# Two stacked graph attentions: graph 0's unmasked attention by product for half of its targets and by prefix tables for the rest, with graph 1's first steps moved ahead of period 0

## The chip, the cores and the metric

The kernel runs on one core of a Trainium2 chip. The metric is the device time of one execution in microseconds (us); the lower the better. All data are float32.

## What is computed

For each of 16 graphs with 1024 nodes of 256 features (one adjacency matrix for all), two layers, each added to its input:

```python
# layer 0 (slope 0.2)
h   = relu(layernorm(x))
out = relu(h @ mlp1_w + mlp1_b)                  # 256 -> 512
res = out
out = gat(relu(out), None, W_fc, a_fc)           # every node attends to every node
out = elu(out) + res
out = relu(out @ mlp2_w + mlp2_b)                # 512 -> 256
res = out
out = gat(relu(out), adj, W_hand, a_hand)        # masked by adj
x   = x + relu(elu(out) + res)
# layer 1 (slope 0.01)
h   = relu(layernorm(x))
x   = x + relu(masked attention of h @ W)

def gat(inp, mask, W, a):
    h = inp @ W
    e = leaky_relu(f1[:, None] + f2[None, :])    # f1 = h @ a[:F], f2 = h @ a[F:]
    return elu(softmax(where(mask, e, -big)) @ h)
```

## The kernel before, in words

A fast path does the whole work; a general path behind a flag is for inputs of a very wide range and does not run here. All line numbers are those of the profile.

**Unmasked attention, two ways.** The weight of source j for target i depends only on f1[i] + f2[j], and leaky_relu has two branches. So if the nodes are sorted by f2, each target's numerator is one prefix sum over the sorted rows of one branch plus one suffix sum of the other. Graphs 1 to 15 do this (class `Dense`): VectorE counts each node's rank (`rank`, L472 to L487), GpSimd scatters the rows of h to their places in memory by indirect DMA (`scatter`, L492), the sync queue reads them back sorted (`read_sorted`, L528), VectorE makes running sums over the eight rows of each partition (`sum_before`, `sum_behind`, L547 to L567), which are written to memory as the fine table (`write_before`, `write_behind`, L557, L570); TensorE adds up the totals of the partitions (`carry`, L578), written as the coarse table. ScalarE finds each target's place by summing signs (`sign`, L516; `count`, L521), GpSimd gathers one fine and one coarse row for each target (`gather`, L589; the coarse gather adds into the fine one's rows), and `share` and `mean` (L599 to L609) divide. Graph 0 doesn't: `vectors`, `query_row`, `weight`, `product`, `product_mean` (L612 to L657) make the 1024 x 1024 weights and multiply them with h on TensorE, eight target tiles of 128 (tile `od`).

**Around it.** `Norm` does the layer norm (statistics `stats`, root `root` on GpSimd, `center`, `turn`: transposes, L250 to L275). `mlp1` (L428), `project` (h for the attention, L442), `merge` and `merge_end` (transposes hpT, elu and the residual add on GpSimd, L664 to L675), `mlp2` (L682). `Masked`, with `Gnn0` and `Gnn1`, is the masked attention of layers 0 and 1: `project` (L309), weights (L354), `product` (tiles oa and ob, L365), `finish`, `combine` (Gnn0's two adds on GpSimd, L387 and L388), `update` (L392, L405).

**Order of the work.** Every step is put into a list with a time of its own by `at(lo, hi, steps)`; the list is sorted by these times and traced in this order, and each engine runs its instructions in the order of the trace. The times are no durations: they only settle the order on each engine. GpSimd's instructions are tied to one another in this order too (L932 to L944), only scatters may stand loosely among themselves. The graphs are staggered: in period b (142 units) TensorE does the first masked product of graph b, the second masked product of graph b - 1, the merges and mlp2 of graph b + 1, and mlp1 and `project` of graph b + 2. Before period 0 stands a prologue (L863 to L899): mlp1 and projection of graph 0, the masks, graph 0's product, its merges and mlp2, mlp1 of graph 1 and its projection, with graph 1's ranks and scatters (`dense_begin`) from 28 units before period 0. Graph 1's sums (`dense_sums`) and gathers (`dense_end`) stand in period 0. Period 0 has no second masked product.

**Buffers.** Tags with few buffers make later tiles wait for earlier ones: "seq" (two: sorted rows, sums, gathered rows, h), "att" (eight weight tiles), "hn" (four), PSUM "mm" (four) and "tr" (two).

The lines that fix the prologue and the stagger:

```python
    base = -1 * PERIOD
    at(base - 6, base + 8, each(d.project, range(NT), [1]))
    at(base + 8, base + 22, each(d.project, range(NT), [0]))
    for t in range(NT):
        lo = base + 40 + 7.1 * t
        at(lo, lo + 7, each(d.product, [t], range(NT)))
    merges(base + 71, d, 0)
    merges(base + 99.2, d, 1)
    second_mlp(base, 0)
    dense_begin(base + PERIOD, 1)
```

Of the kernel before, what the change touches and what calls it, by code (L numbers as in the profile page):

```python
# [8 lines left out]
F32 = mybir.dt.float32  # L9
# [22 lines left out]
def fast_path(ctx: ExitStack, tc: tile.TileContext, alarm, x, adj, w1, b1, w2, b2, w_fc, a_fc,  # L32
# [49 lines left out]
    def load_x(b, name):  # L82
        xt = big.tile([P, NT, F], F32, tag="x", name=f"{name}_{b}", bufs=3)
        nc.sync.dma_start(xt, x[b].rearrange("(t p) f -> p t f", p=P))
        return xt
# [284 lines left out]
    class Gnn0(Masked):  # L370
        ONES = 2

# [10 lines left out]
        def combine(self, t, o_nat):  # L383
            e, pos = self.out[t]
            nc.scalar.activation(e, e, AF.Exp, scale=-1.0)
            nc.scalar.activation(e, e, AF.Exp, bias=neg1)  # L386
            nc.gpsimd.tensor_add(pos, pos, o_nat[:, t, :])  # L387
            nc.gpsimd.tensor_add(e, e, pos)  # L388
            self.out[t] = e
# [21 lines left out]
    class Dense:  # L411


        def __init__(self, b):
# [6 lines left out]
            self.dens = {}  # L421

# [96 lines left out]
        def count(self):  # L519
            self.k = k = small.tile([P, 2, NT], I32, tag="k", name=f"k_{self.b}")  # L520
            nc.vector.tensor_scalar(k[:, 0, :], self.signs, -0.5, N / 2, op0=OP.mult, op1=OP.add)  # L521
            nc.vector.tensor_scalar(k[:, 1, :], k[:, 0, :], 3, None, op0=OP.arith_shift_right)

        def read_sorted(self):
            self.xs = big.tile([P, NT, R], F32, tag="seq", name=f"xs_{self.b}", bufs=2)
            rows = sorted_d[self.b % 2].rearrange("(p r) f -> p r f", p=P)
            for h in range(2):
                reader = nc.sync.dma_start(self.xs[:, half(h)], rows[:, half(h)])  # L528
# [4 lines left out]
        def sums_begin(self):  # L533
            b = self.b
            self.bd = small.tile([P, 2, NT], F32, tag="bd", name=f"bd_{b}")
            self.tt = big.tile([P, NT, K], F32, tag="seq", name=f"tt_{b}", bufs=2)
            self.all_t = work.tile([P, K], F32, tag="part", name=f"all_{b}")
            nc.gpsimd.memset(self.tt[:, 0, :], 0.0)

        def sums_weights(self, h):  # L540
            f2 = self.xs[:, half(h), K]
# [5 lines left out]
        def sum_before(self, r):  # L547
            xs, bd, tt = self.xs, self.bd, self.tt
            if r == 0:
                nc.vector.tensor_scalar(tt[:, 1, :], xs[:, 0, :K], bd[:, 1, 0:1], None, op0=OP.mult)  # L550
            else:
                nc.vector.scalar_tensor_tensor(tt[:, r + 1, :] if r + 1 < NT else self.all_t,
                                               xs[:, r, :K], bd[:, 1, r:r + 1], tt[:, r, :],
                                               op0=OP.mult, op1=OP.add)

        def write_before(self):
            nc.sync.dma_start(fine_d[self.b % 2][:N, :K].rearrange("(p r) f -> p r f", p=P),  # L557
                              self.tt)

        def sum_behind(self, r):  # L560
            xs, bd = self.xs, self.bd
            if r == NT - 1:
                nc.vector.tensor_scalar(xs[:, r, :K], xs[:, r, :K], bd[:, 0, r:r + 1], None,
                                        op0=OP.mult)
            else:
                nc.vector.scalar_tensor_tensor(xs[:, r, :K], xs[:, r, :K], bd[:, 0, r:r + 1],  # L566
                                               xs[:, r + 1, :K], op0=OP.mult, op1=OP.add)  # L567

        def write_behind(self):
            nc.sync.dma_start(fine_d[self.b % 2][:N, K:].rearrange("(p r) f -> p r f", p=P),  # L570
                              self.xs[:, :, :K])

        def carry(self, s):
            lhsT, total = ((upto, self.all_t), (after, self.xs[:, 0, :]))[s]
# [9 lines left out]
        def gather(self, h, coarse, u):  # L584
            if h not in self.got:
                self.got[h] = big.tile([P, TH, 2 * K], F32, tag="seq", name=f"got_{self.b}_{h}",
                                       bufs=2)
            t = h * TH + u
            nc.gpsimd.indirect_dma_start(  # L589
                out=self.got[h][:, u, :], out_offset=None,  # L590
# [4 lines left out]
        def share(self, h):  # L595
            got = self.got[h]
            qh = self.q[:, h * TH:(h + 1) * TH]
            den = self.dens[h] = small.tile([P, 2, TH], F32, tag="den", name=f"den_{self.b}_{h}")
            nc.vector.tensor_mul(den[:, 0, :], got[:, :, F], qh)  # L599
            nc.vector.tensor_add(den[:, 0, :], den[:, 0, :], got[:, :, K + F])  # L600
            nc.vector.reciprocal(den[:, 0, :], den[:, 0, :])
            nc.vector.tensor_mul(den[:, 1, :], den[:, 0, :], qh)

        def mean(self, h, u):
            got, den, name = self.got[h], self.dens[h], f"{self.b}_{h}_{u}"
            part = work.tile([P, K], F32, tag="part", name=f"part_{name}")
            nc.scalar.activation(part, got[:, u, :K], AF.Copy, scale=den[:, 1, u:u + 1])
            hp = self.hps[h, u] = work.tile([P, K], F32, tag="hp", name=f"hp_{name}", bufs=TH)
            nc.vector.scalar_tensor_tensor(hp, got[:, u, K:], den[:, 0, u:u + 1], part,  # L609
                                           op0=OP.mult, op1=OP.add)  # L610

        def vectors(self):  # L612

            b, f1, f2 = self.b, self.fs[:, 0, :], self.fs[:, 1, :]
            ext_ps = tr_psum(f"extdps_{b}")
            row_broadcast(ext_ps[:, :P], [self.ext])
            top = small.tile([P, 3], F32, tag="topd", name=f"topd_{b}")
            nc.vector.tensor_reduce(top[:, 0:1], ext_ps[:, :P], AX.X, OP.max)
            nc.vector.tensor_scalar(top[:, 1:2], top[:, 0:1], -1.0, None, op0=OP.mult)
            nc.vector.tensor_scalar(top[:, 2:3], top[:, 0:1], -SLOPE_A, None, op0=OP.mult)  # L620
            self.q = small.tile([P, NT], F32, tag="qd", name=f"qd_{b}")
            nc.vector.tensor_scalar(self.q, f1, top[:, 0:1], 0.0, op0=OP.add, op1=OP.max)
            nc.scalar.activation(self.q, self.q, AF.Exp, scale=SLOPE_A - 1.0)
# [762 lines left out]
```

## Time and profile before

| | us |
|---|---|
| median of 3 runs | 2419.56 (2419.07 to 2420.93) |
| the profiled execution | 2418.14 |
| its span in the trace | 2416.4 |
| TensorE busy | 2331.7 |
| VectorE busy | 1611.9 |
| ScalarE busy | 1280.2 |
| GpSimd busy | 965.5 |

The profile is one execution. In the 40 slices of the span a digit is the busy share of a slice in tenths, and PEclk is the granted TensorE clock in tenths. In rows of a timeline stand start, duration, engine, line, operation, out<-in, the number of instructions (x), and in brackets the idle time before and what ended it. A float32 matmul of the program shows as two records. A name such as oa or hpT leaves out the buffer numbers: oa is graph b's first masked product, ob its second, od graph 0's unmasked one, nt a norm's transposes, m an mlp's sum. Times that follow each other on an engine overlap by some tenths of a microsecond.

### The profile page before, as it was taken

How to read it: one execution, taken by the hardware profiler on the slowest of the kernel's cores; microseconds unless marked ns; L12 is line 12 of the kernel's file. 1: busy time of each engine (PE TensorE's matmuls, PEld its weight loads, DVE VectorE, ACT ScalarE, POOL GpSimd, SP SyncE). 2: the span in 40 equal slices, each digit the busy share in tenths (PEclk: the TensorE clock that was granted, in tenths of full speed). 3: DMA queues.
4: the chain of work that ended last, by engine and by line, in shares of the span. 5: the costliest groups of instructions: out<-in, count | busy, mean ns of one | idle time of the engine just before them, and what ended most of it. 6: DMA issues, size and time to landing. Idle time of an engine off the chain costs nothing. (4 is left out here: it accounts for less than half of the span.)

```text
span 2416.4 us, 31367 instructions
## 1 busy us (share of the span) xinstructions
PE 2331.7 (96%) x10393; PEld 1809.2 (75%) x10393; DVE 1611.9 (67%) x4455; ACT 1280.2 (53%) x2723; POOL 965.5 (40%) x1214
## 2 busy tenths in 40 slices
PE   7999699999999999999999999999999999999897
PEld 5777478787887878788787778878777787878666
DVE  6247377685866768586676858667685866758554
ACT  4236454565655456564545656454565645455442
POOL 1013436344353634435363443536344353634320
PEclk9999799999999999999999999999999999999898
DMA  5005637255472725547272554727265472726500
GB/s 183 1 1 156 167 108 193 75 175 132 149 192 106 192 78 172 134 147 194 100 193 79 172 139 138 203 96 195 77 172 143 140 201 88 197 75 186 129 1 28
DMA packets 139067, 320.50 MB, mean 133 GB/s; under 512 B 9224, under 2 KB 60424, under 8 KB 135056
## 3 DMA queue, kind: packets, MB, share of 16 engines
q0 software_dynamic: 44160, 157.68, 24.2%
q1 hardware_dynamic: 94736, 160.72, 22.9%
q8 instruction: 85, 1.39, 0.2%
q14 instruction: 86, 0.70, 0.1%
HBM read 199.08 MB, written 119.29 MB: 132 GB/s over the span
## 5 line engine op out<-in xcount | busy, mean ns | idle before, releaser
L365 PE MATMUL oa<-hma,atta 128*128 128x258 f32 x2048 | 460.0, 384 | 8.1 <-DVE atta L354 4.7
L365 PE MATMUL ob<-hmb,attb 128*128 128x257 f32 x2048 | 458.3, 383 | 5.5 <-DVE attb L354 5.5
L442 PE MATMUL h<-wfc_sb,resT 128*128 128x257 f32 x2048 | 463.5, 380 | 0.0
L365 PEld LDWEIGHTS oa<-hma,atta 128*128 128x128 f32 x2048 | 385.5, 191 | 73.7 <-DVE atta L354 10.8
L365 PEld LDWEIGHTS ob<-hmb,attb 128*128 128x128 f32 x2048 | 391.2, 192 | 61.6 <-ACT hmb L349 3.7
L442 PEld LDWEIGHTS h<-wfc_sb,resT 128*128 128x128 f32 x2048 | 379.2, 189 | 51.8 <-issue 0.5
L675 POOL TENSOR_TENSOR resT<-resT,e 128x512 f32<-128x512 f32 x128 | 162.7, 1271 | 506.8 <-DVE e L674 456.6
L354 DVE SCALAR_TENSOR_TENSOR atta<-rowsa,qwda,edge 128x256 f32<-128x256 f32 x512 | 252.5, 521 | 40.4 <-ACT rowsa L345 33.3
L354 DVE SCALAR_TENSOR_TENSOR attb<-rowsb,qwdb,edge 128x256 f32<-128x256 f32 x512 | 257.2, 531 | 30.9 <-PE ob L365 20.2
L387 POOL TENSOR_TENSOR posa<-posa,onat 128x256 f32<-128x256 f32 x128 | 107.3, 839 | 414.8 <-ACT posa L380 414.6
L428 PE MATMUL m<-hT,w_sb 128*128 128x512 f32 x512 | 236.9, 597 | 0.0
L682 PE MATMUL m<-resT,w_sb 128*128 128x512 f32 x512 | 229.7, 596 | 2.4 <-POOL resT L675 2.4
L589 POOL DMA_INDIRECT got<-coarse,k x120 | 187.8, 1565 | 36.6 <-issue 36.6
L401 ACT ACTIVATE rb<-ob,recb 128x256 f32<-128x256 f32 x128 | 57.4, 474 | 269.3 <-DVE recb L399 259.5
L666 DVE TENSOR_SCALAR e<-hpT 128x512 f32<-128x512 f32 x128 | 88.5, 691 | 156.1 <-PE hpT L664 155.3
L682 PEld LDWEIGHTS m<-resT,w_sb 128*128 128x128 f32 x512 | 94.2, 191 | 103.5 <-issue 95.3
L444 ACT COPY hnat<-h 128x257 f32<-128x257 f32 x256 | 92.2, 366 | 147.7 <-PE h L442 130.0
L379 ACT ACTIVATE ea<-oa,reca 128x256 f32<-128x256 f32 x128 | 60.5, 473 | 184.7 <-DVE reca L376 184.7
L388 POOL TENSOR_TENSOR ea<-ea,posa 128x256 f32<-128x256 f32 x128 | 118.6, 927 | 91.4 <-ACT ea L386 70.2
L428 PEld LDWEIGHTS m<-hT,w_sb 128*128 128x128 f32 x512 | 92.2, 192 | 81.3 <-issue 80.5
L589 POOL DMA_INDIRECT got<-fine,k x120 | 128.7, 1073 | 38.2 <-issue 35.1
L516 ACT ACTIVATE junk<-r,fs 128x1024 int8<-128x1024 f32 x120 | 137.6, 1147 | 1.5
(181 smaller groups left out, 3609.1 us busy)
## 6 DMA issues: line engine op xcount, KB each, us to landing
xs<-sorted SPq DMA_DIRECT2D x30, 1028.0 KB
fine<-tt SPq DMA_DIRECT2D x15, 2052.0 KB
fine<-xs SPq DMA_DIRECT2D x15, 2052.0 KB
xn<-in_x_dram SPq DMA_DIRECT2D x16, 1024.0 KB
x<-in_x_dram SPq DMA_DIRECT2D x16, 1024.0 KB
out_dram<-x SPq DMA_DIRECT2D x32, 512.0 KB
coarse<-carry SPq DMA_DIRECT2D x30, 256.5 KB
adj<-in_adj_dram SPq DMA_DIRECT2D x1, 2048.0 KB
```

The lines of the kernel that those rows point to most:

```text
L354: nc.vector.scalar_tensor_tensor(a_t, self.rows[:, q * PAIR:(q + 1) * PAIR], self.qwd[:, 1, j:j + 1], edge[:, j, q * PAIR:(q + 1) * PAIR], ...
L365: nc.tensor.matmul(self.out[t][:, :F + self.ONES], lhsT=self.att[q, j][:, (t % 2) * P:(t % 2 + 1) * P], rhs=self.hm[:, j, 2:2 + F + self.O ...
L387: nc.gpsimd.tensor_add(pos, pos, o_nat[:, t, :])
L388: nc.gpsimd.tensor_add(e, e, pos)
L428: nc.tensor.matmul(ps, lhsT=w1_sb[:, kc, c * P:(c + 1) * P], rhs=hT[:, kc, h * HALF:(h + 1) * HALF], start=(kc == 0), stop=(kc == FC - 1))
L442: nc.tensor.matmul(ps[:, :F + 1], lhsT=self.resT[:, kc, t * P:(t + 1) * P], rhs=wfc_sb[:, kc, g, :], start=(kc == 0), stop=(kc == HC - 1))
L444: nc.scalar.copy(self.h_nat[:, t, g, :], ps[:, :F + 1])
L516: nc.scalar.activation(junk, self.r2, AF.Sign, bias=self.fs[:, 0, t:t + 1], accum_out=self.signs[:, t:t + 1])
L589: nc.gpsimd.indirect_dma_start(out=self.got[h][:, u, :], out_offset=None, in_=(coarse_d if coarse else fine_d)[self.b % 2][:, :], in_offse ...
L666: nc.vector.tensor_scalar_min(e, ps, 0.0)
L675: nc.gpsimd.tensor_add(dst, dst, e)
L682: nc.tensor.matmul(ps, lhsT=w2_sb[:, kc, c * P:(c + 1) * P], rhs=self.resT[:, kc, h * HALF:(h + 1) * HALF], start=(kc == 0), stop=(kc == H ...
```

## The change

Graph 0 takes target tiles 0 to 3 by the product and tiles 4 to 7 by tables: it gets the steps that the other graphs have (`row`, `rank`, `scatter`, `read_sorted`, sums, `carry`, gathers, `share`, `mean`), for half of the signs and gathers. Its tables lie in tiles of half size under other tags ("onat", "x", "hm"). In the prologue graph 1's projection of the f2 half, its ranks, its scatters, its sums and its signs come ahead of period 0, and its gathers into the first half of it. The order of period 0 is new: graph 2's mlp1 second half follows the masked product, then the norm, in whose midst half of graph 0's second projection stands; graph 0's adds in `combine` go from GpSimd to VectorE; statistics stand earlier. All periods from 1 on begin 28 units earlier in the list. The first x is loaded in two halves. In every period but the last two, the scales of Gnn1 stand two units earlier.

```diff
     def load_x(b, name):
-        nc.sync.dma_start(xt, x[b].rearrange("(t p) f -> p t f", p=P))
+        src = x[b].rearrange("(t p) f -> p t f", p=P)
+        for part in ((slice(0, TH), slice(TH, NT)) if name == "xn" and b == 0 else (slice(0, NT),)):
+            nc.sync.dma_start(xt[:, part], src[:, part])
...
     class Gnn0(Masked):
+        beside_gathers = False
...
-            nc.gpsimd.tensor_add(pos, pos, o_nat[:, t, :])
-            nc.gpsimd.tensor_add(e, e, pos)
+            adder = nc.vector if self.beside_gathers else nc.gpsimd
+            adder.tensor_add(pos, pos, o_nat[:, t, :])
+            adder.tensor_add(e, e, pos)
...
     class Dense:
+            self.split = b == 0
...
         def count(self):
+            some = slice(TH if self.split else 0, NT)
...
         def read_sorted(self):
+            if self.split:
+                self.xs = [big.tile([P, TH, R], F32, tag=tag, name=f"xs_{self.b}_{h}", bufs=bufs)
+                           for h, (tag, bufs) in enumerate((("onat", 1), ("x", 3)))]
...
         def sums_begin(self):
+            if self.split:
+                self.tt = [big.tile([P, TH, K], F32, tag="hm", name=f"tt_{b}_{h}", bufs=2)
+                           for h in range(2)]
...
         def gather(self, h, coarse, u):
+                n, tag = (2, "hm") if self.split else (TH, "seq")
+                self.got[h] = [big.tile([P, n, 2 * K], F32, tag=tag, name=f"got_{self.b}_{h}_{i}",
+                                        bufs=2) for i in range(TH // n)]
...
+    gnn0[0].beside_gathers = True
...
     def first_norm(t0, b):
-        at(t0 - 29.5, t0 - 28.5, n.stats_steps(0))
+        lo = t0 - (62 if b == 2 else 29.5)
+        at(lo, lo + 1, n.stats_steps(0))
-        n.turn_at(t0 - 22, 0, 4)
+        n.turn_at(t0 - (14.5 if b == 2 else 22), 0, 4)
...
     def first_mlp(t0, b):
-        at(t0 + 78.1, t0 + 85, steps[HC:])
+        lo = t0 + (39.3 if b == 2 else 78.1)
+        at(lo, lo + 7, steps[HC:])
...
     def second_norm(t0, b):
+        elif b == 0:
+            n.turn_at(t0 + 47, 0)
+            n.turn_at(t0 + 50.5, 1, 1.6)
+            lo = t0 + 47.2
...
-            at(lo + 42, lo + 54, each(m.scale, range(NT)))
-            at(lo + 102.5, lo + 102.5, [m.row])
+            at(lo + 40, lo + 52, each(m.scale, range(NT)))
+            at(base_of(b + 1) + 31.5, base_of(b + 1) + 31.5, [m.row])
...
+    SHORT = 28.0
+    def base_of(b):
+        return b * PERIOD - SHORT * (b > 0)
+    START = -168.0
+    at(START + 33, START + 50, each(d.project, range(NT), [1]))
+    n.turn_at(START + 64, 0, 18)
+    n.turn_at(START + 66, 1, 1.7)
+    at(START + 50.5, START + 64, each(d.project, range(NT), [0]))
+    at(START + 54.2, START + 54.2, [d.row])
+    at(START + 54.5, START + 71, each(d.rank, range(NT)))
+    scatters(d, START + 56.5, START + 73)
+    at(START + 74, START + 74, [d.read_sorted])
+    at(START + 66.6, START + 80, mlp_steps(1))
+    at(START + 71.2, START + 80, each(d.sign, tiles(1)))
+    at(START + 80, START + 94, each(dense[1].project, range(NT), [1]))
+    at(START + 76, START + 82, each(d.weight, [0], range(NT)))
...
+    at(START + 100, START + 100, each(d.carry, range(2)))
+    for t in range(TH):
+        lo = START + 95 + 7.1 * t
+        at(lo, lo + 7, each(d.product, [t], range(NT)))
+        at(lo + 8.2, lo + 8.2, [partial(d.product_mean, t)])
+    at(START + 100, START + 107, each(d.weight, [1], range(NT)))
+    gathers(d, 1, START + 108, START + 114)
+    e = dense[1]
+    at(START + 99, START + 118, each(e.rank, range(NT)))
+    merges(START + 125, d, 0)
+    at(START + 135, START + 135, [partial(d.share, 1)])
+    at(START + 135.5, START + 137, each(d.mean, [1], range(TH)))
+    merges(START + 138.2, d, 1)
+    second_mlp(START + 39, 0, -13)
+    at(START + 123.4, START + 141, each(e.project, range(NT), [0]))
+    scatters(e, START + 126, START + 142)
+    first_norm(0, 2)
+    at(START + 144, START + 158, each(e.sign, range(NT)))
...
     for b in range(NB):
+            for h in range(NH):
+                lo = base + (16 if b == 0 else 48 + 4 * h)
+                gathers(dense[b + 1], h, lo + 12 * h, lo + 6 + 12 * h) if b == 0 else gathers(
+                    dense[b + 1], h, lo, base + 58 + 7 * h)
```

## Prediction

> **What bounds the kernel now.** I read the page first (the busy table and the 40 slices), then the engines by stretches of 60 us, then TensorE in order of time through the first 500 us, then the other engines where TensorE stands still.
>
> ```profile
> span 2416.4 us, 31367 instructions
> PE 2331.7 (96%) x10393; PEld 1809.2 (75%) x10393; DVE 1611.9 (67%) x4455; ACT 1280.2 (53%) x2723; POOL 965.5 (40%) x1214
> PEclk9999799999999999999999999999999999999898
> ```
>
> TensorE is the bound; the one dip away from the end is slice 5 (240 to 300 us), where its clock is 7 tenths too. By stretches (columns: TensorE, its weight loads, VectorE, ScalarE, GpSimd, clock, DMA share, GB/s):
>
> ```profile
> 60.00:120.00 60.00, 58.27 (x258) 44.55 (x258) 17.50 (x49) 14.61 (x27) 2.84 (x10) 1.00 0.00 1
> 120.00:180.00 60.00, 59.79 (x264) 45.93 (x264) 26.31 (x70) 18.80 (x35) 11.92 (x17) 1.00 0.00 1
> ...
> 240.00:300.00 60.00, 40.04 (x159) 29.80 (x160) 20.42 (x50) 25.65 (x54) 29.74 (x27) 0.77 0.72 171
> 300.00:360.00 60.00, 59.70 (x257) 42.85 (x256) 41.27 (x129) 34.87 (x75) 19.01 (x36) 1.00 0.27 100
> ```
>
> So from 60 to 205 us only removed TensorE work shortens the run, while VectorE is 29 and 44% busy and the DMA queues are empty. In 240 to 300 us the waits themselves can go. TensorE in order of time:
>
> ```profile
> 63.29 0.60 PE L270 MATMUL nt<-ident,hn 128*128 128x128 f32 x4
> ...
> 84.06 30.70 PE L646 MATMUL od<-hnat,attd 128*128 128x257 f32 x140
> ...
> 205.18 21.66 PE L365 MATMUL oa<-hma,atta 128*128 128x258 f32 x98
> ...
> 240.00 1.95 PE L578 MATMUL carry<-xs,after 128*128 128x257 f32 x4 [3.78 <-DVE stats L250]
> 245.82 1.97 PE L270 MATMUL nt<-ident,hn 128*128 128x128 f32 x8 [3.87 <-DVE hn L260]
> 254.25 1.94 PE L270 MATMUL nt<-ident,hn 128*128 128x128 f32 x8 [6.46 <-DVE hn L260]
> 278.54 0.66 PE L234 MATMUL extpsb<-ident,extb 128*128 128x128 f32 x2 [9.63 <-DVE extb L317]
> ...
> 348.84 21.05 PE L365 MATMUL oa<-hma,atta 128*128 128x258 f32 x96
> ...
> 490.19 21.05 PE L365 MATMUL oa<-hma,atta 128*128 128x258 f32 x96
> ```
>
> The masked product of graphs 0, 1 and 2 begins at 205.18, 348.84 and 490.19: period 0 took 143.66 us, period 1 took 141.35, although period 0 has no second-layer product of an earlier graph (128 records of 0.218 = 27.9; 0.218 is the start-to-start of the od row, 84.06 to 114.59 for 140) and no second-layer row (0.9). Its work is 141.35 - 28.8 = 112.6, so 31.0 us are lost: 25.2 idle (with the two waits at 227.99 and 232.47) and about 5.8 in which the halved clock stretches records. The 9.63 is VectorE's:
>
> ```profile
> 276.00 0.16 DVE L599 TENSOR_TENSOR den<-got,qd 128x4 f32<-128x4 f32 x1 [20.84 <-DMA got<-coarse,k]
> ```
>
> extb stands behind den in VectorE's order, and den waits for graph 1's gathers, which GpSimd began at 248.65.
>
> **The change, part by part.**
>
> *Half of the product.* Four of eight od tiles go: 4 x 8 x 2 matmuls of two records, 128 x 0.218 = 27.9 us. Added on TensorE: the row of f2 (eight transposes, 0.9) and the carries (eight records, 1.13 x 2 by period 1's rows, 2.3 with their evictions). Net -24.7, all on the path.
>
> *The start.* x of graph 0 comes in two halves. The full load let VectorE begin at 6.57; the windows show 0.2 MB moved by 3 us and 330 GB/s behind it, so the first half should be there at about 5.0. The centers then stand in order (before, hn 4 stood ahead of hn 2 and waited for GpSimd's root until 12.60). Eight stats and two constants (8 x 0.53 + 0.4) end at 9.7, centers 0 to 3 at 11.1; the transposes of the second half wait for the evictions (2 x 0.54) and end at 13.2. mlp1 starts at 13.3 instead of 17.23: -3.9 (bounds -2 to -4.5).
>
> *Ranks beside graph 1's norm (a new wait).* mlp1, masks and both projections took 63.29 - 17.23 = 46.1; with the row of f2 inside (1.0), graph 1's first transposes come at 60.4 and the row at 50.7. Ranks can start after its eviction (1.0) and top (0.6) at 52.5. Eight ranks took 171.30 to 188.46 with four centers among them: 15.7, or 1.96 each. Centers 6 and 7 of graph 1 now stand behind rank 5: 52.5 + 6 x 1.96 + 4 x 0.35 = 65.7. The last transposes could have ended at 62.1, so TensorE stands some 4 us; before, the same place cost 67.64 - 63.29 - 1.74 = 2.6. Net +1.4 (0 to +5). Here a rule of the Trainium skill speaks against the change: "TensorE: Matmul & The Clock Gate" (Part 1, the HAM clock gate, and Part 4, PE-mode transpose) says that about 3.4 us of idleness halve the clock and that transposes do not count as activity. By that, 5.6 us of transposes and waiting alone would halve the next 3.4 us, +1.7. The row: 63.29 to 67.64 was also only transposes, 4.35 us, and the stretch 60 to 120 has clock 1.00; after the full 3.78 us stand at 240 it was 0.53. I take 0, since the wait comes in pieces under 2 us, and keep +2 in the range.
>
> *Waits in the rest of the prologue.* od begins at 66.1 + 14.7 (67.64 to 82.36) + 8 x 1.74 = 94.7. The ranks of graph 1 now stand among the weights of the second pair, which wait for od's buffers: rank 0, then weights until 105, and so on; the second tile's eviction comes behind rank 4 at about 119.7, and the fourth tile needs its PSUM at 117.8: +2 (0 to 4).
>
> *Tables of graph 0.* They need 13 MB of DMA in a stretch that moved 1 GB/s, and VectorE's 12 us of sums. Last rank 69.6, scatters land at 73, read by 80 (the read at 198.04 gave the first half by about 203), sums 82.6 to 96, the second table lands 10 us after its issue, 106.5 (231.18 to about 241.5). GpSimd could gather then, but ahead of the gathers in its order stands graph 2's root, which waits for stats that VectorE reaches behind rank 3 and the weights, at 117: gathers start at 118.4. Four fine ones (0.53 MB each, 6.3 us) and four coarse (2.6 us each: eight took 264 to 285) and 2 us latency: 137. Share, four means at 0.72 to 0.75: 142.5. od with the rows inside it (0.9 + 0.1 + 2.3, and 1.8 for b2's column sums) and that wait ends at 94.7 + 27.9 + 5.1 + 2 = 129.7, and TensorE wants hp at 129.7 + 7 x 1.74 + 4 x 0.43 = 143.6, or 141.6 without the wait: +1 (0 to +15, see rivals). Behind these gathers on GpSimd stand graph 1's scatters and the residual adds of graph 0: 8 x (0.35 + 1.15) + 4 x 1.27 from 131 gives 148, against 143 at which TensorE ends h. Sorted rows are back at 154 to 157; ScalarE's signs (8 x 1.27) stand ahead of the sum weights, and graph 2's centers 4 to 7 stand between the sums: 170 to 171.5, where TensorE wants them at 167.5 to 168.5. +3 (0 to 8).
>
> Prologue: -24.7 - 3.9 + 1.4 + 2 + 1 + 3 = -21.2, so oa begins near 184.
>
> *Period 0.* Graph 1's sums and signs are out of it. Gathers start when the second table has landed, about 189, and end their issue at 216 (8 x 1.25 + 8 x 1.84 = 24.7 and two roots); the results lie by about 226, wanted at 228 and, for the second half, 242. mlp1's second half (6.9) and half of pb (3.5) now cover the last norm: 11.2 us with the transposes. The chain is rec, relu, two exps, two adds, update, stats, root, center: the last period's took 2352.05 to 2365.4, 13.3 us, of which 2.5 stood behind an update that waits for GpSimd's adds and 2.3 on GpSimd; with the adds on VectorE about 10 to 12.5. I leave 1.5 us of new waits (0 to 8) and recover 29.5 of the 31.0; the clock loss goes with the waits.
>
> *Adds on VectorE.* 16 adds, 0.33 to 0.43 each by x<-x,rb: 5 to 7 us, on VectorE, which in that stage then has 26 of 30 us. "SBUF — State Buffer" of the Trainium skill (Who interferes with whom) says that a VectorE operation with two SBUF inputs and a GpSimd one that reads SBUF exclude each other for whole instructions. A gather's issue reads its indices there: by that each add could stand up to 1.55 us behind one, 25 us, and the stage would be VectorE's. The rows say otherwise: from 389 to 404 GpSimd issued ten gathers and VectorE's weights and adds with two SBUF inputs took 0.42 to 0.48, their usual time, while beside GpSimd's adds an update took 0.93 instead of 0.41. I take the rows: free.
>
> *Steady periods.* TensorE's order from graph 2 on is the same; ScalarE scales two tiles earlier, under cover of 10 us of projection: 0 (-1 to +1 over all).
>
> Sum: -21.2 - 29.5 = -50.7. The profiled execution took 2418.14 (span 2416.4 and 1.7 around it); the median is 2419.56. 2419.56 - 50.7 = 2369; I say **2368**.
>
> **Rivals.** *A, as above* (0.60): 2360 to 2377. *B, the gap moves into the prologue* (0.24): graph 0's gathers are late. In steady state the row's eviction (312.27) to den (418.70) takes 106 us; here I allow 86. At 106, TensorE stands 20 us before hpT and the clock halves for some 4 more: -51 + 20 + 2 gives 2390; half of it 2379. For it: three engines' orders meet in that chain, and the root ahead of the gathers. Against: 106 holds pauses in which the step wasn't due. *C, the waits hide each other* (0.11): a late TensorE meets nothing that is late; -24.7 - 3.9 - 2.6 - 31 gives 2357. *D, slower* (0.02): the same chain past its limit. Gathers, residual adds, graph 1's scatters and its gathers are one queue on GpSimd; each us that graph 0's coarse gathers are late reaches TensorE whole. It takes 51 us, den at about 190 instead of 139, before the kernel is slower; at 200, 2430. Nothing in the rows makes a gather that slow. The rest (0.03) lies between B and D; no change (within 0.2%, 4.8 us, about what a measurement can tell) is 0.01 of it.
>
> The range reaches down to C's middle and up to B's lower half, 2356 to 2383; beyond it lie about 0.05 below and 0.14 above.
>
> **What would show it.** od with half its records; mlp1 beginning at 13 to 14; oa of graph 0 at 180 to 188; between it and oa of graph 1 112 to 118 us at full clock; waits of 3 to 5 us on hn before graph 1's norm and 2 to 4 before graph 2's second half; graph 0's gathers beginning near 118, behind the root. Wrong: a wait over 6 us before hpT (B), clock under 0.9 in 180 to 300, or periods from graph 2 on that differ from 141.35.

## The result, and the profile after the change

The changed kernel takes 2392.24 us (median of 4 runs, 2388.57 to 2395.08) against 2419.64 (2419.07 to 2420.93) for the kernel before beside it: a ratio of 0.9885, with an interval of 0.9868 to 0.9902. It is 27.4 us faster; 50.7 were forecast, and 2392 lies 9 us above the upper end of the range. The profiled execution took 2395.08, its span 2393.4.

The span, the busy row and the clock of the page, and then the stretches of 60 us:

```profile
span 2393.4 us, 31270 instructions
PE 2311.4 (97%) x10281; PEld 1788.2 (75%) x10281; DVE 1635.3 (68%) x4531; ACT 1286.1 (54%) x2740; POOL 977.9 (41%) x1216
PEclk9999999999999999999999999999999999999898
```

```profile
60.00:120.00 60.00, 56.25 (x232) 41.60 (x231) 41.80 (x134) 20.71 (x45) 8.03 (x15) 0.94 0.58 164
120.00:180.00 60.00, 52.10 (x218) 37.43 (x216) 38.40 (x95) 30.45 (x58) 33.22 (x44) 0.94 0.48 141
180.00:240.00 60.00, 51.80 (x220) 38.15 (x218) 34.79 (x100) 29.98 (x72) 18.36 (x17) 0.98 0.89 216
240.00:300.00 60.00, 54.16 (x230) 39.22 (x231) 35.81 (x99) 32.07 (x65) 19.81 (x26) 0.91 0.20 39
```

TensorE's busy time fell by 20.3 us, and the dip in slice 5 of the clock is gone. But the stretches from 60 to 180, which had clock 1.00 and almost no idle time, now have 0.94 and 11.7 us of idle time, and 180 to 300 is not whole either: 14 us idle, clock 0.98 and 0.91. TensorE in order of time, at the places that the prediction named (start, duration, what ran, and in brackets the wait before it and what ended it):

```profile
14.30 10.92 PE L434 MATMUL m<-hT,w_sb 128*128 128x512 f32 x20
...
65.85 0.67 PE L272 MATMUL nt<-ident,hn 128*128 128x128 f32 x4 [1.85 <-DVE hn L262]
68.39 1.12 PE L272 MATMUL nt<-ident,hn 128*128 128x128 f32 x4 [1.87 <-DVE hn L262]
69.30 9.01 PE L434 MATMUL m<-hT,w_sb 128*128 128x512 f32 x16
...
150.57 0.30 PE L686 MATMUL hpT<-ident,hp 128*128 128x128 f32 x1 [1.57 <-DVE hp L639]
151.14 0.33 PE L686 MATMUL hpT<-ident,hp 128*128 128x128 f32 x1 [0.27 <-DVE hp L639]
153.21 0.48 PE L686 MATMUL hpT<-ident,hp 128*128 128x128 f32 x1 [1.74 <-DVE hp L639]
153.87 0.47 PE L686 MATMUL hpT<-ident,hp 128*128 128x128 f32 x1 [0.19 <-DVE hp L639]
154.14 3.63 PE L448 MATMUL h<-wfc_sb,resT 128*128 128x257 f32 x8
...
169.29 1.12 PE L704 MATMUL m<-resT,w_sb 128*128 128x512 f32 x2 [1.14 <-POOL resT L697]
171.34 1.12 PE L704 MATMUL m<-resT,w_sb 128*128 128x512 f32 x2 [0.93 <-POOL resT L697]
...
195.00 1.91 PE L367 MATMUL oa<-hma,atta 128*128 128x258 f32 x8
...
243.73 1.76 PE L272 MATMUL nt<-ident,hn 128*128 128x128 f32 x6 [10.42 <-DVE hn L262]
...
246.81 5.69 PE L311 MATMUL pb<-wl_sb,hT 128*128 128x258 f32 x16 [0.47 <-ACT hT L276]
...
324.17 6.04 PE L367 MATMUL oa<-hma,atta 128*128 128x258 f32 x27
```

The masked product of graph 0 begins at 195.00 instead of 205.18, where 184 was forecast: the prologue gave 10.2 us of 21.2. That of graph 1 begins at 324.17: period 0 takes 129.2 instead of 143.66, where 114.2 was forecast, so it gave 14.5 of 29.5. The rest of the run is as long as before (2069.2 us to the end of the span against 2067.6, with steady periods of 141.2 to 142.3). Two kinds of loss are to be seen: small waits, and behind each group of them records at half clock. A usual set of 16 m records takes 7.03 us and of 8 h records 1.90; here they take 9.01 and 3.63. The largest wait is 10.42 us, before graph 0's transposes in period 0. Those stand behind hn, hn needs graph 0's norm roots (rstd), and these run on GpSimd:

```profile
214.90 1.11 POOL L615 DMA_INDIRECT got<-fine,k  x1 [33.10 <-DVE reca L379]
...
238.39 1.56 POOL L615 DMA_INDIRECT got<-coarse,k  x1 [5.05 <-DMA got<-fine,k]
240.25 1.54 POOL L615 DMA_INDIRECT got<-coarse,k  x1 [0.30 <-issue]
241.26 0.83 POOL L257 TENSOR_SCALAR rstd<-mv 128x4 f32<-128x4 f32 x1
```

The statistics that the first root needs were complete at 222.6 on VectorE, but in GpSimd's order it stands behind 14 of graph 1's 16 gathers, and they began at 214.90, 26 us later than forecast: 11 because the prologue was longer, and the rest because the first gather went 24 us after the issue of the second fine table (190.86), where the sum allowed 10. Among the gathers themselves stands one more wait, the 5.05 us before the fifth coarse one: a coarse gather adds into rows that a fine one brings, and these had not landed. Without it the root would have run some 5 us sooner (an estimate from these rows).

### The profile page after: what moved, and what is told of

The parts are those of the page before. It is cut to its first block, busy times and chain, and to the rows that moved or that the text cites. A ratio compares the mean times of both kernels' runs of the same rounds, so it can differ in the third digit from the quotient of the medians.

```text
span 2393.4 us, 31270 instructions
## 1 busy us (share of the span) xinstructions
PE 2311.4 (97%) x10281; PEld 1788.2 (75%) x10281; DVE 1635.3 (68%) x4531; ACT 1286.1 (54%) x2740; POOL 977.9 (41%) x1216
## 5 line engine op out<-in xcount | busy, mean ns | idle before, releaser
L391 POOL TENSOR_TENSOR posa<-posa,onat 128x256 f32<-128x256 f32 x120 | 101.0, 841 | 390.2 <-ACT posa L383 390.2
L615 POOL DMA_INDIRECT got<-coarse,k x124 | 195.6, 1577 | 42.5 <-issue 36.2
L615 POOL DMA_INDIRECT got<-fine,k x124 | 135.6, 1093 | 68.4 <-DVE reca L379 33.1
L498 POOL DMA_INDIRECT sorted<-hnat,place x128 | 131.8, 1030 | 39.3 <-issue 16.3
L392 POOL TENSOR_TENSOR ea<-ea,posa 128x256 f32<-128x256 f32 x120 | 112.1, 934 | 85.0 <-ACT ea L389 67.4
```

The source lines that it names most:

```text
L391: adder.tensor_add(pos, pos, o_nat[:, t, :])
L392: adder.tensor_add(e, e, pos)
L498: made = nc.gpsimd.indirect_dma_start(out=sorted_d[self.b % 2], out_offset=bass.IndirectOffsetOnAxis(ap=self.place[:, t:t + 1], axis=0), i ...
L615: nc.gpsimd.indirect_dma_start(out=got[u // n][:, u % n, :], out_offset=None, in_=(coarse_d if coarse else fine_d)[self.b % 2][:, :], in_o ...
```

## The experiments

**Theory 1** (period 0): the wait is due to the place of graph 0's roots behind late gathers, and the gathers are late because loads of x share the DMA queues with the tables. Its rivals: the norm chain with the adds on VectorE is itself too long; something on VectorE holds the gathers (the row of 214.90 names reca, VectorE's, as what came last). **Theory 2** (prologue): what is missing are small waits that three engines' orders make, and the half clock that follows each group of them. Its rival: graph 0's gathers are late, rival B of the prediction. Where nothing else is said, each kernel is the changed one with one edit, and its ratio is to the kernel before on the same chip.

**p0_roots.** The roots ahead of graph 1's second eight gathers:

```diff
-                gathers(dense[b + 1], h, lo + 12 * h, lo + 6 + 12 * h) if b == 0 else gathers(
+                gathers(dense[b + 1], h, lo + 21 * h, lo + 6 + 25 * h) if b == 0 else gathers(
```

> Changed kernel, only GpSimd's order in period 0 altered: graph 0's two norm roots stand ahead of graph 1's second eight gathers (the first root after 8 gathers instead of 14, the second after 12 instead of 16). Theory 1 (the 10.42 us wait before graph 0's transposes in period 0 is the roots' place behind the gathers): the wait falls under 2 us, the half clock behind it (5.69 for 16 pb records instead of 3.65, about 4 us in all) goes too, the gathers still begin near 215; 10 to 14 us faster than the changed kernel, about 2380. Rival (the adds on VectorE and the two exponentials of ScalarE make the norm chain itself late): the wait stays over 5 us and the gain is under 5.

It took 2381.73 us (2380.96 to 2383.20), ratio 0.9851 (0.9835 to 0.9868). Period 0 went from 129.2 to 118.8 us. GpSimd and TensorE there:

```profile
211.90 1.11 POOL L615 DMA_INDIRECT got<-fine,k  x1 [33.03 <-DVE reca L379]
...
223.97 0.84 POOL L257 TENSOR_SCALAR rstd<-mv 128x4 f32<-128x4 f32 x1
```

```profile
230.88 0.76 PE L272 MATMUL nt<-ident,hn 128*128 128x128 f32 x4 [0.48 <-DVE hn L262]
...
233.74 5.44 PE L311 MATMUL pb<-wl_sb,hT 128*128 128x258 f32 x16 [0.58 <-ACT hT L276]
```

The gathers begin as late as before (19.8 us after oa), the root runs as soon as its statistics are there, and 10.42 became 0.48 (with 0.22 and 0.41 behind it). That is theory 1's first half; the chain through the adds was not too long. The half clock did not go with the wait in this execution (5.44 for 16 pb records instead of the usual 3.81): some 3 us of transposes and small waits are still in front of them.

**p0_loads.** Graph 0's second load of x and graph 3's first one issued near 108 us, behind graph 0's coarse table:

```diff
-        at(t0 + 3, t0 + 3, [partial(load_again, b)])
+        if b:
+            at(t0 + 3, t0 + 3, [partial(load_again, b)])
...
-            at(lo, lo, [partial(load_first, b + 3)])
+            if b:
+                at(lo, lo, [partial(load_first, b + 3)])
...
+    at(START + 101, START + 102, [partial(load_again, 0), partial(load_first, 3)])
```

> Changed kernel, only two loads moved: graph 0's second load of x and graph 3's first load (1 MB each) are issued behind graph 0's coarse table, near 108 us, instead of at 180.7 and 200.4 us beside graph 1's tables. Theory 1 (graph 1's gathers begin at 214.9, 24 us after its second table is issued, because the DMA engines carry 6.7 MB from 180 to 214): the second table lands some 10 us sooner, gathers begin at about 205, the wait before the transposes falls from 10.4 to 1 to 3 us, 8 to 11 us faster. Rival (something on VectorE or in the order holds the gathers): they still begin at 214 to 215 and the time stays within 2 us.

2386.45 us (2379.82 to 2390.03), ratio 0.9861 (0.9845 to 0.9878). The first gather came at 207.82, 14.3 us behind the start of oa instead of 19.9, and 18.5 behind the issue of the second table instead of 24.0. The wait fell from 10.42 to 5.37, period 0 to 124.9. So the loads do hold the gathers, but for 5.6 us and not for 10. That VectorE does not hold them is shown by rc_adds, below: there it did nothing from 204.7 to 216.5, and the first gather began at 210.06 all the same, 20.1 us behind oa as in the changed kernel, with the table named as what it waited for.

**roots_loads.** Both edits together:

> Changed kernel with the roots ahead of the second eight gathers and the two loads moved to 108 us. Theory 1 (the late gathers cost only through the roots that stood behind them): with the roots ahead nothing waits for the gathers any more, so the loads are worth nothing on top: the time equals that of the roots alone within 1.5 us and period 0 stays at 118.8. Rival (late gathers still reach TensorE through den and hp of graph 1): another 2 to 4 us faster, period 0 near 115.

2382.81 us (2375.41 to 2384.05), ratio 0.9847 (0.9828 to 0.9867): the same as the roots alone. Its first gather comes 11.5 us behind oa, 8 sooner than in p0_roots, and nothing is won by it. Period 0 took 117.1 where p0_roots took 118.8, but this time its 16 pb records ran at full clock (3.81 instead of 5.44), which is the whole difference, and without these loads it was 117.4 too (roots_centers, below). Late gathers cost only through the roots behind them.

**pro_centers.** Graph 1's four centers together on VectorE, ahead of graph 0's rank 5:

```diff
-    n.turn_at(START + 66, 1, 1.7)
+    n.turn_at(START + 66, 1, 2.6)
```

> Changed kernel, only VectorE's order in the prologue altered: all four centers of graph 1's second half stand together, behind graph 0's rank 4 and ahead of its rank 5 (before, two stood behind rank 4 and two behind rank 5). Theory 2 (two pieces of waiting, 1.85 and 1.87 us, with only transposes between them, halve TensorE's clock for 16 records at 69.3, 9.01 instead of 7.03): one piece of 1.85 stays, the other goes; if the pieces add up for the clock, the half clock goes as well: 3.5 to 4 us faster. If the clock had fallen for another reason (one piece is enough): 1.9 faster and the 16 records still take about 9. Rival (the time is made up later, at the hp wait or the sums): no gain, the waits behind od's end grow by what is won.

Its trace shows one wait of 1.85 less, and the records behind it at full clock:

```profile
65.34 1.35 PE L272 MATMUL nt<-ident,hn 128*128 128x128 f32 x8 [1.85 <-DVE hn L262]
66.53 7.03 PE L434 MATMUL m<-hT,w_sb 128*128 128x512 f32 x16
```

oa of graph 0 begins at 190.3, against 192.1 to 195.0 in six traces with the old order. Pieces of waiting add up for the clock when only transposes lie between them: before the edit TensorE did nothing but transposes from 62.96 to 69.30, 6.3 us, here from 62.46 to 66.53, 4.1 us. In the time alone it does not show: 2389.77 us (2384.10 to 2391.12), ratio 0.9886 (0.9869 to 0.9902), inside what these kernels scatter. It is priced by roots_centers, below.

**pro_hp.** Graph 0's gathers ahead of graph 2's root, and the denominators earlier on VectorE:

```diff
-    gathers(d, 1, START + 108, START + 114)
+    at(START + 100.5, START + 101, each(d.gather, [1], [0], range(TH)))
+    at(START + 101, START + 102, each(d.gather, [1], [1], range(TH)))
...
-    at(START + 135, START + 135, [partial(d.share, 1)])
+    at(START + 130, START + 130, [partial(d.share, 1)])
```

> Changed kernel, in the prologue only: graph 0's gathers stand ahead of graph 2's norm root on GpSimd (so they need not wait for VectorE's statistics at 122.8), and the denominators (share) stand five units earlier on VectorE, ahead of the last two merges. Rival B of the prediction (late gathers are what makes hp late): gathers begin near 110, hp is ready as soon as its buffers are free, the waits before hpT (3.8 us) and the half clock behind them (2 to 2.5) go, 5 to 6 us faster. Theory 2 (gathers have nothing to do with it; VectorE's den took 1.84 and hp 4.14 because GpSimd's scatters and adds run beside them): only the denominators' place is won, hp still takes about 4 for four, the wait falls by 1 to 2.5 and the gain is 1 to 3.

2393.59 us (2388.31 to 2394.79), ratio 0.9892 (0.9876 to 0.9909): nothing. The gathers began at 115.72 instead of 124.36, sooner than the 118.4 of the forecast; the denominators were complete at 145.35 instead of 149.76. But hp began only at 148.58 (149.68 before), behind the last step of a merge on VectorE and a part of ScalarE's, and four took 4.43 us; the waits before hpT were 3.9 in all (3.8 before), and oa began at 194.4. Rival B is out: the gathers of graph 0 were not what was late. Even theory 2 had expected 1 to 3 us.

**ctl_after.** The changed kernel once more, unedited:

> The changed kernel itself once more, as the reference on this chip for the kernels beside it: 0.9885 of before, 2388 to 2395, and again 10.4 us of waiting before graph 0's transposes in period 0. Both theories expect the same; what it tells is how far the time at which oa of graph 0 begins (192 to 195 in four kernels with the same start) moves from run to run.

2391.98 us (2387.25 to 2394.09), ratio 0.9886 (0.9869 to 0.9902); oa at 193.9, the wait in period 0 9.29.

**roots_centers.** The two reorderings together:

> Changed kernel with both reorderings that removed a wait: graph 0's norm roots ahead of graph 1's second eight gathers, and graph 1's four centers together. If the two losses lie one behind the other on TensorE (theory 1 with theory 2): the gain is their sum, 10.4 and 3 to 4, and period 0 stays at 118.8: 13 to 15 us faster than the changed kernel, about 2377. Rival (an earlier oa meets tables that are still late, so that the gathers or the hp of graph 1 come into the path): period 0 grows by 1 to 4 us and the gain over the roots alone is under 1.

2378.06 us (2377.55 to 2379.59), ratio 0.9836 (0.9820 to 0.9853), 13.9 under ctl_after on the same chip. oa begins at 190.0, period 0 takes 117.4. The losses add up. The centers are worth some 3.7 us of it (against p0_roots; the intervals of these two overlap).

**start_only.** The kernel before, with the first load in halves and the centers in order:

```diff
-        nc.sync.dma_start(xt, x[b].rearrange("(t p) f -> p t f", p=P))
+        src = x[b].rearrange("(t p) f -> p t f", p=P)
+        for part in ((slice(0, TH), slice(TH, NT)) if name == "xn" and b == 0 else (slice(0, NT),)):
+            nc.sync.dma_start(xt[:, part], src[:, part])
...
-    n.turn_at(base - 21.5, 1, 2)
+    n.turn_at(base - 20, 1, 1.7)
...
```

> The kernel before with one part of the change alone: x of graph 0 loaded in two halves, and the centers of its second half in order behind the first half's. The prediction's step said 3.9 us (mlp1 at 13.3 instead of 17.23). The changed kernel's trace: mlp1 at 14.30, which is 2.9, but its first 20 records took 10.92 instead of 9.30 at half clock. Theory 2: mlp1 at 14.3, the first records 9.4 to 10.9 long, and the time 1.3 to 2.8 us less than before. Rival (what is won at the start is lost at graph 1's centers or the empty stretch behind): the time stays within 1 us of before.

2416.60 us (2412.23 to 2417.89) against 2418.64, ratio 0.9992 (0.9985 to 0.9999): 2.0 us, not 3.9. mlp1 begins at 14.17. Its trace also shows the place on which the prediction had rested its case against the clock rule, unchanged work some 2 us earlier, and this time at half clock. First the kernel before, then start_only:

```profile
66.82 0.98 PE L270 MATMUL nt<-ident,hn 128*128 128x128 f32 x7 [0.16 <-ACT hT L274]
67.64 1.88 PE L428 MATMUL m<-hT,w_sb 128*128 128x512 f32 x4
```

```profile
64.71 1.75 PE L272 MATMUL nt<-ident,hn 128*128 128x128 f32 x7 [0.16 <-ACT hT L276]
66.26 2.79 PE L430 MATMUL m<-hT,w_sb 128*128 128x512 f32 x4
```

Up to these seven transposes, the pause of transposes and small waits had lasted 3.5 us in both.

**rc_scatters.** roots_centers, with all of graph 1's scatters behind graph 0's first four residual adds on GpSimd:

```diff
-    scatters(e, START + 126, START + 142)
+    scatters(e, START + 140.2, START + 140.6)
```

> The kernel with both reorderings (roots and centers, 2378.06, oa of graph 0 at 190.0), and GpSimd's scatters of graph 1 moved behind graph 0's first four residual adds, all eight together. There den's second addition took 1.86 us instead of 0.16 and four hp 4.13, with a GpSimd add of 1.28 beside each. Theory 2 (VectorE's den and hp stand still while a GpSimd add holds the port that the two share): with the adds done by then, den takes 0.16, four hp about 3.0, the four waits before hpT (3.9 us) fall to 1 to 1.5: 2.5 us faster, oa at 187 to 188. If the scatters' own issue holds the port as well, hp stays near 4 and only den's 1.7 is won. Rival (hp is late because the gathers land late): no change.

2379.86 us (2378.71 to 2380.13), ratio 0.9846 (0.9830 to 0.9863): no gain, but both halves can be seen. VectorE's den and hp in order of time, in roots_centers and then here:

```profile
141.99 1.86 DVE L628 TENSOR_TENSOR den<-den,got 128x2 f32<-128x2 f32 x1
...
144.16 4.13 DVE L639 SCALAR_TENSOR_TENSOR hp<-got,den,part 128x513 f32<-128x513 f32 x4
```

```profile
142.25 0.94 DVE L630 TENSOR_TENSOR den<-den,qd 128x2 f32<-128x2 f32 x1
...
143.98 3.19 DVE L639 SCALAR_TENSOR_TENSOR hp<-got,den,part 128x513 f32<-128x513 f32 x4
```

The waits before hpT fell from 3.9 to 2.25; the eight h records behind them still took 3.27 us, at half clock. But the next residual adds now stood behind the eight scatters, and these behind a copy that waits for the last projection tile, so TensorE lost it all again at one place:

```profile
163.10 5.59 PE L704 MATMUL m<-resT,w_sb 128*128 128x512 f32 x8 [4.15 <-POOL resT L697]
```

**rc_ends.** roots_centers, with each of graph 0's second merges ended ahead of the next one on VectorE, and ScalarE's signs of graph 1 later:

```diff
-    merges(START + 138.2, d, 1)
+    at(START + 138.2, START + 147.4, each(d.merge, [1], range(HC)))
+    at(START + 140.3, START + 149.5, each(d.merge_end, [1], range(HC)))
...
-    at(START + 144, START + 158, each(e.sign, range(NT)))
+    at(START + 150, START + 164, each(e.sign, range(NT)))
```

> The kernel with both reorderings, and in graph 0's second merges the end of each merge ahead of the next one's first step on VectorE, with ScalarE's signs of graph 1 six units later. There TensorE waited 1.15 and 0.92 for resT near 163 and 165. Theory 2 (the third residual add is late because its VectorE step stands behind the next merge's, the fourth because a sign of 1.13 stands ahead of its exponential on ScalarE): the first wait goes, the second shrinks to about 0.4, 1.5 us faster. Rival (GpSimd's scatters ahead of the adds are what makes them late, as the first reading of the trace had it): both waits stay.

2376.76 us (2374.09 to 2379.72), ratio 0.9831 (0.9815 to 0.9848): not to be told from roots_centers. The first wait went, the second grew from 0.92 to 1.86, and a new one of 1.23 stood before pa. From the last hpT to the last add there are five steps on three engines, and TensorE has only six m records to lay over them: the 2 us follow from this chain's own length, and only the first wait was VectorE's order.

**rc_adds.** roots_centers, with graph 0's sixteen adds back on GpSimd:

```diff
-    gnn0[0].beside_gathers = True
+    gnn0[0].beside_gathers = False
```

> The kernel with both reorderings, and graph 0's sixteen adds back on GpSimd (that part of the change undone). Theory (the adds on VectorE are free, and on GpSimd they would stand behind gathers that wait for graph 1's tables until 20 us after oa begins): the first add comes 7 to 9 us later, TensorE waits for ScalarE or for the norm, and period 0 grows from 117.4 by 3 to 8 us: 2381 to 2386. Rival (the adds cost the norm chain as much on VectorE as they would on GpSimd): period 0 stays within 1.5 us of 117.4.

2392.91 us (2390.24 to 2396.62), ratio 0.9906 (0.9890 to 0.9923): some 15 us slower than roots_centers. Period 0 is 135.2, 17.8 longer, where 3 to 8 were expected. The mechanism is the one named, with one more member: VectorE waits for a sum that GpSimd makes behind the gathers (the first line, VectorE's), and TensorE's next weights stand behind that wait on VectorE (the second, TensorE's):

```profile
216.51 0.93 DVE L396 SCALAR_TENSOR_TENSOR x<-ea,x 128x256 f32<-128x256 f32 x1 [11.81 <-POOL ea L392]
```

```profile
218.35 10.75 PE L367 MATMUL oa<-hma,atta 128*128 128x258 f32 x40 [7.22 <-DVE atta L356]
```

**rc_scatters2.** roots_centers, with six scatters behind the four residual adds and ahead of the last two copies, and two behind these:

```diff
-    scatters(e, START + 126, START + 142)
+    scatter_steps.append(e.scatter)
+    at(START + 135.5, START + 136, each(scatter_steps[-1], range(6)))
+    at(START + 139.5, START + 140, each(scatter_steps[-1], range(6, NT)))
```

> The kernel with both reorderings, and graph 1's scatters in two groups on GpSimd: six behind graph 0's first four residual adds, two behind the copies of the last two projection tiles (with all eight there, hp took 3.19 us for four and TensorE waited 2.25 before hpT instead of 3.9, but 4.15 for the next residual adds, which stood behind the scatters). Theory 2 (a GpSimd add beside den and hp holds VectorE's port; a scatter's issue does so little): hp takes 3.2 to 3.6, the waits before hpT come to 2.3 to 2.8, the waits for resT stay near 2, oa begins near 188 and the time is 1 to 2 us under 2378. Rival (a scatter's issue holds the port as an add does): hp takes about 4 again, nothing is won and the time stays at 2378 or above.

2370.18 us (2368.74 to 2375.21, 5 runs), ratio 0.9809 (0.9795 to 0.9822): the best of all, 47 us under the kernel before and, by the ratios, 18 under the changed one. oa begins at 185.5. In order of time, TensorE behind the last hp, and then GpSimd beside VectorE's hp:

```profile
146.64 0.33 PE L686 MATMUL hpT<-ident,hp 128*128 128x128 f32 x1 [0.55 <-DVE hp L639]
146.81 1.90 PE L448 MATMUL h<-wfc_sb,resT 128*128 128x257 f32 x8
```

```profile
144.39 1.31 POOL L498 DMA_INDIRECT sorted<-hnat,place  x1 [0.30 <-issue]
146.01 1.42 POOL L498 DMA_INDIRECT sorted<-hnat,place  x1 [0.31 <-issue]
```

Four hp took 3.18, the waits before hpT 2.25 instead of 3.9, those for resT stayed at 2.06. That is the 1.7 us that was expected; the other 3 come from the clock of this execution. In roots_centers the eight h records behind the last hp took 3.46, two m records 1.86 and eight transposes 1.91; here 1.90, 1.13 and 1.04, and the stretch from 120 to 180 has clock 1.00.

The shorter wait alone does not explain that: rc_scatters had the same waits of 2.25 and lost the clock behind them. What differs is where the pause lies. In all fourteen traces the granted clock changes only on a grid of 3.413 us, counted from the first grant of full clock: every stretch of one clock but the last is a whole multiple of it. The pause of 3.5 us in rc_scatters fills most of one cell of the grid, and the next cell is at half clock; the pause of 3.4 us in rc_scatters2 is shared by two cells, each with more matmuls in it, and none is. The cells in rc_scatters, and then in rc_scatters2:

```profile
143.43:146.84 3.41, 1.54 (x6) 0.59 (x4) 2.95 (x7) 2.74 (x5) 0.65 (x3) 1.00 0.00 0
146.84:150.26 3.42, 3.04 (x8) 2.48 (x9) 1.02 (x2) 1.35 (x2) 0.00 (x0) 0.50 0.00 0
```

```profile
141.94:145.35 3.41, 2.12 (x9) 1.23 (x8) 3.05 (x8) 2.66 (x6) 2.89 (x5) 1.00 0.20 76
145.35:148.76 3.41, 2.44 (x12) 1.99 (x13) 1.80 (x3) 1.37 (x3) 2.74 (x3) 1.00 0.43 160
```

So a part of the 3 us is luck. Not all of it: the mean granted clock of the five runs is 0.992 to 0.994, that of the four of roots_centers 0.989 to 0.992.

## Why the prediction was wrong, point by point

The largest step that failed is in period 0: the norm roots were counted into the time of the gathers that stand ahead of them, as if nothing waited for a root, and TensorE waited 10.4 us for the first. In the prologue three terms failed: the half clock behind waits, taken as 0, cost some 6 us; the wait before hpT, taken as 1, was 3.8; the wait for the residual adds, not in the sum, was 2.1.

**The work.** TensorE's busy time fell by 20.3; the steady periods did not change. The half product, the row and the carries were costed rightly, and so was the work of the prologue: in roots_centers od ends at 128.7 (forecast 129.7) and graph 1's norm at 65.75 (66.1). Part of the 24.7 was eaten by clock, as follows.

**The start** (-3.9). The first half of x was there as forecast (4.86), but the 16 transposes, at half clock, take 1.97 and 2.24 us a set of eight, where the sum took some 1 us: mlp1 begins at 14.2 to 14.5 instead of 13.3. Then its first 20 records take 9.28 to 10.92 us, by execution. Alone the part is worth 2.0.

**The clock behind waits** (taken as 0). This step failed by its reasoning. "TensorE: Matmul & The Clock Gate" of the Trainium skill (Part 1, the HAM clock gate, and Part 4, PE-mode transpose) was weighed against one row of one execution and rejected, since waits "in pieces under 2 us" should not count. They do: with both pieces, 16 m records took 9.01, 8.73, 8.73, 8.73, 8.27 and 8.00 us in six traces with the old order; with one piece, 7.03 in all six with the new. And the row could not decide it: in start_only the same pause, 3.5 us up to that place, halved the clock. The page says that the window of activity is free-running; the grid of 3.413 us in the traces agrees. Where a pause lies in it would then decide, and the two kernels with moved scatters bear that out. The grid begins at the first grant of full clock, which came anywhere from 15.24 to 18.66 us. In the changed kernel's trace the clock was lost at four places: at the start (up to 1.6), at graph 1's norm (2.0), behind hp (some 2.5) and behind period 0's wait (2.0).

**The wait before hpT** (+1). The gathers began at 124.4, 6 us later than forecast, but TensorE was not waiting for them: pro_hp rules rival B out, though its 2390 lies next to what was measured. (The items given for this chain come to about 141 us, not 142.5.) Of the 3.8 us, 1.7 come from GpSimd's residual adds beside den and hp: 1.86 instead of 0.16, ending with the add, and 4.13 instead of 3.2. The other 2.25 stayed when the adds were out of the way; hp then stands behind the last merges on VectorE and ScalarE's parts, and no run tried to shorten that. "SBUF — State Buffer" (Who interferes with whom) was set aside by rows in which VectorE ran beside GpSimd's gathers. For adds on GpSimd that rule agrees with the rows, which show the standing still and not the port that the expectations speak of; beside a scatter it was the scatter that stretched (0.97 to 1.42). The prediction had itself a row with an update of 0.93 beside a GpSimd add, and used it only for the other case. The 1 should have been 3.8.

**Residual adds** (+0). 2.1 us, of which the sum had nothing. The scatters ahead of them are not the reason, as the first reading had it: the waits stay when the scatters are moved (2.06 in rc_scatters2), GpSimd stands idle 2.7 us before the third add in roots_centers, and 1.86 stay when VectorE's order is changed (rc_ends). A cover is gone. Before the change, 16 h records of graph 1 (3.63 us), graph 0's row and the first m records lay between the last hpT and the m that need the last sums:

```profile
163.62 0.60 PE L664 MATMUL hpT<-ident,hpd 128*128 128x128 f32 x4
164.06 3.63 PE L442 MATMUL h<-wfc_sb,resT 128*128 128x257 f32 x16
```

The change has moved these h records ahead, and the sum counted them as moved work, not as what hid a chain of some 5 us. This is read from the two timelines; no run put the cover back.

**Graph 2's centers** (+3). No wait came; this was too careful.

Together: 1.0 and 1.6 at the start, 2.0, 2.8, 2.5 and 2.1, less 3, and 1 more in small waits between od and hpT: 10.0 of the 11.0 us by which oa was late.

**Period 0** (-29.5). The failing words are "(8 x 1.25 + 8 x 1.84 = 24.7 and two roots)": the roots were counted into the gathers' time, and it was not asked who waits for them. With gathers done by 216 they would have been free, so the table's landing (24 us instead of 10) had to fail as well, and 5 us came from a coarse gather that waited for its fine rows, of which the sum had nothing. 10.4 us by p0_roots; with 2.0 of half clock and about 3 us in pieces where 1.5 was left, these make most of the 15.0. Of the landing, the loads explain 5.6 to 8.4; where the rest comes from was not tried.

**The adds** (free on VectorE). Right, and worth more than was said: rc_adds shows 15 us, because on GpSimd they would stand behind gathers that wait.

What confirms the account: with three orders changed and no work taken away, rc_scatters2 comes to 2370.18 (2373 by its ratio), and 2368 was forecast. Its prologue is 1.5 us longer than forecast and its period 0 4.6; that it comes nearer than their sum is in part chance, since from oa of graph 1 to the end it took 2062.7, where the changed kernel took 2069.2 for the same code.

## What to carry to other kernels

When steps are moved onto an engine that had been idle, write out that engine's order with the instruction that each one waits for, and ask of every short instruction in it (a root, a copy, an add) who waits for it: here three reorderings on GpSimd and VectorE were worth as much as two thirds of the change itself. Count small waits with transposes between them as one pause, and price a pause of some 3 us or more at its own length and up to some 2 us of half clock behind it, which one execution may pay and the next not. And do not reject a rule by one row of one execution where its outcome can differ from run to run.

## What the runs showed of the hardware that was not expected

- The clock's cost is drawn anew in each execution. The grid of 3.413 us began at 15.24 us in one trace (roots_centers), where the first 20 m records took 9.28 us, and at 18.66 in another (the changed kernel), where they took 10.92. The same 36 ob records of graph 14 took 8.04 (pro_centers, rc_scatters2), 9.68 (ctl_after) or 10.34 (start_only), and the last period 138.4 to 143.5. The scatter of a kernel's runs goes with it: 2388.57 us at a mean granted clock of 0.990 and 2395.08 at 0.987 in the changed kernel, 2408.45 at 0.991 and 2420.59 at 0.986 among 23 runs of the kernel before on one chip.
- A pause of 3.4 us with transposes left the clock whole behind hp (rc_scatters2), one of 3.5 at the same place halved it (rc_scatters), and so did one of 5.1 (roots_centers).
- Two fine tables written 10.8 us apart let the first gather go 24 us after the second's issue, and 15.6 to 18.5 with 2 MB of loads out of the way, where they were written 12.0 and 10.8 us apart; written 17.8 us apart, in the kernel before, the second seemed to land in about 10. What sets the rest was not tried.
